# Attention values: six half-width products, three of them on 64 of the 128 rows of TensorE

## The chip, the cores and the metric

The kernel runs on one NeuronCore of a Trainium2 chip. The metric is the device time of one execution in microseconds (us). All data are fp32. The engines have short names in the profile: PE is the matrix engine (TensorE), PEld its weight loads, DVE the VectorE, ACT the ScalarE, POOL the GpSimd engine, and SP the engine whose queue issues the DMAs.

## The reference

The kernel computes one macaron block over 4 sequences of 256 tokens with 512 features: a feed-forward part at half weight, an attention part, and the feed-forward part again. Cut to what matters here:

```python
x = x + 0.5 * ffn(layernorm(x))
# attention, 32 query heads, 8 key/value heads of 128, window of 128 tokens
q, k = rope(x_n @ wq), rope(x_n @ wk);  v = x_n @ wv
allowed = (j <= i) & (j > i - 128)
attn = softmax(where(allowed, q @ k.T * sm_scale, neg))
x = x + (attn @ v) @ wo
x = x + 0.5 * ffn(layernorm(x))
```

The change is in the line `attn @ v`.

## The kernel before, in words

The tokens are worked on in two halves `h` of two sequences `b` each. For every half and every key/value head `g` there is a group of four query heads; each of the 16 groups has two units (b = 0 and b = 1), so there are 32 units. The projections are done in Strassen's manner: seven products of half size and additions on DVE and POOL (`sums_a`, `sums_b`, `queries`, `keys`, `project_values`, `outputs`). The order of PE, DVE, POOL and ACT instructions is written out by hand for most of the kernel: for each unit the main loop runs the steps of the next group's queries (letters in `order`), the scores of the next unit, the output products of the previous unit (`late`), the mask, and `values` at the end. DMAs are issued by SP in an order of the scheduler's.

In a unit, the queries of one sequence (256 tokens) are cut into 8 blocks of 32 tokens. `scores` makes scores, `exponentials` and `normalize` the softmax weights in `probs`; the window is folded, so that a query block of tokens 128 to 255 has only 128 key columns: the column of key `k` holds the weight of key `k` or of key `k + 128`, whichever the window allows. `turn_blocks` transposes 32x32 blocks on DVE and writes them to DRAM (`kept`); `fetch` reads them back into `turned` with four DMAs, so that keys lie on the 128 partitions and (head, query block, query) on the free axis. That leaves, for each key partition, 512 columns for the first 128 query tokens and 512 for the second.

`split` (L804) copies the second 512 columns into `part` with the weights of the first key tile set to zero. It runs on POOL for b = 0 and in the last group (an affine select, L807), otherwise on DVE (a product with the constant mask `new`, L812). `difference` (L817) has replaced the value tile v1 by v1 - v0. `values` (L822) then makes three products of 128 rows and 512 columns each (L829): the first 512 columns with v0 into the bank `oa`, the second 512 with v0 and `part` with v1 - v0 into the bank `ob`. ACT copies each bank to `oT` as soon as it is done (L832); `oT` is read by four additions on POOL (`oTs`, L126) and by the output products `y` on PE (L852), which come in the next unit.

Other names in the prediction: L739 and L753 are the score products `sa` and `sb`, L575 the query products, L742 the masks and maxima of the scores on DVE, L531 the last sum of a rope on POOL, L554 additions of Strassen parts on DVE, L462, L464 and L485 sums of the feed-forward part, `wq`, `wk` and `wv` weight tiles that SP loads.

Of the kernel before, what the change touches and what calls it, by code (L numbers as in the profile page):

```python
# [12 lines left out]
F32 = mybir.dt.float32  # L13
AF = mybir.ActivationFunctionType
ALU = mybir.AluOpType
AX = mybir.AxisListType

P = 128
B, S, D = 4, 256, 512
T = B * S  # L20
NT = T // P
NH, NKV, HD = 32, 8, 128
G = NH // NKV
# [15 lines left out]
def macaron_kernel(  # L39
# [154 lines left out]

    def by_heads(dst, make):
        make(dst, 0)
        other = sb.tile(list(dst.shape), F32, tag="by_heads", bufs=1, name=f"{dst.name}_hi")
        for j in range(1, G):
            make(other, j * BLK)
            nc.gpsimd.tensor_copy(dst[ts(j, BLK), :], other[ts(j, BLK), :])  # L200
# [35 lines left out]
    for c in range(1, NB):  # L236
        nc.gpsimd.memset(turned[ts(c, BLK), :, :c, :], 0.0)


    old = const.tile([P, NB, BLK], F32, name="old")  # L240
    nc.gpsimd.memset(old, 1.0)
    nc.gpsimd.affine_select(
        out=old, in_=old, compare_op=ALU.is_gt,
        fill=0.0, base=0, pattern=[[-BLK, NB], [-1, BLK]], channel_multiplier=1,
    )
    new = const.tile([P, NB, BLK], F32, name="new")
    nc.gpsimd.tensor_scalar(new, old, -1.0, 1.0, ALU.mult, ALU.add)

    rank = const.tile([P, E], F32, name="rank")
    for e in range(E):  # L250
# [103 lines left out]
    def ffn(tiles, tag, then):  # L354
# [22 lines left out]
        def narrow(i):  # L377
            t = tiles[i]
            if i == 0:
                state["hl"] = sb.tile([P, TPH, E * R + E], F32, tag="hl", name=f"hl_{tag}_{t0}")[:, :n, :]  # L380
            pa = score_bank(f"pa_{tag}_{t}")
            for c in range(KC):
                nc.tensor.matmul(  # L383
                    pa[:, : E * R + E], x_of(i, c), ar_sb[:, c, :],
                    start=(c == 0), stop=(c == KC - 1),
                )
            nc.scalar.copy(state["hl"][:, i, :], pa[:, : E * R + E])
# [165 lines left out]
    def add(dst, bank, other):  # L553
        nc.vector.tensor_tensor(dst, bank, other, ALU.add)  # L554
# [111 lines left out]
    def project_values(h, g):  # L666


        x, w = xs[h], weights["vs", h, g]
        dst = sb.tile([P, TPH, 2 * HD], F32, tag="v", name=f"v_{h}_{g}")  # L670
        vS[h, g] = dst
        banks = [mm_bank(f"v{n}_{h}_{g}").rearrange("p (b i f) -> p b i f", b=BPH, i=2) for n in range(2)]
        (c11, c12), (c21, c22) = ((bank[:, 0], bank[:, 1]) for bank in banks)
        (v11, v12), (v21, v22) = (
            (dst[:, :2, cols], dst[:, 2:, cols]) for cols in (slice(0, HD), slice(HD, 2 * HD))
        )
        p1c, u2, v1 = (
            temp(n, f"v_{h}_{g}")[:, :S].rearrange("p (i f) -> p i f", i=2) for n in ("p1c", "u2", "v1")
        )

        def product(n, bank, start=False):
            for i in range(2):
                for c in range(2):
                    nc.tensor.matmul(  # L684
                        bank[:, i, :], x[n - 1][:, c, i, :], w[n - 1][:, c, :],
                        start=(start and i == 0 and c == 0), stop=(c == 1), skip_group_check=True,
                    )

        def first():
            product(1, c11, True)  # L690
            nc.scalar.copy(p1c, c11)
            product(6, c22, True)

        def both():
            add(u2, c22, p1c)

        def second():
            product(5, c12)
            add(v1, c12, u2)
            product(7, c21)  # L700
            add(v22, c21, v1)

        def others():
            product(2, c11)
            product(4, c21)
            add(v21, c21, u2)
            product(3, c12)
            nc.scalar.copy(v11, c11)
            add(v12, c12, u2)
            difference(h, g)  # L710

        return first, both, second, others

# [82 lines left out]
    def fetch(name):  # L796
        heads = kept.pop(name).rearrange("(j k) c x -> k j c x", j=G)
        for c in range(NB):
            nc.sync.dma_start(
                out=turned[ts(c, BLK), :, c:, :].rearrange("p j n q -> p j (n q)"),  # L800
                in_=heads[:, :, c, c * BLK :],
            )

    def split(h, g, b):  # L804
        part = sb.tile([P, G, NB, BLK], F32, tag="part", bufs=1, name=f"part_{h}_{g}_{b}")
        if b == 0 or (h, g) == groups[-1]:
            nc.gpsimd.affine_select(  # L807
                out=part, in_=turned[:, :, NB:, :], compare_op=ALU.is_ge, fill=0.0, base=0,
                pattern=[[0, G], [BLK, NB], [1, BLK]], channel_multiplier=-1,
            )  # L810
        else:
            nc.vector.tensor_tensor(  # L812
                part, turned[:, :, NB:, :], new.unsqueeze(1).to_broadcast([P, G, NB, BLK]), ALU.mult
            )
        return [turned[:, :, :NB, :]], [turned[:, :, NB:, :], part]

    def difference(h, g, tiles=slice(None)):  # L817

        pairs = vS[h, g].rearrange("p (b i) f -> p b i f", i=2)[:, tiles]
        nc.vector.tensor_tensor(pairs[:, :, 1], pairs[:, :, 1], pairs[:, :, 0], ALU.subtract)  # L820

    def values(h, g, b, p0, p1):  # L822
        oT = sb.tile([HD, G, S], F32, tag="oT", bufs=4, name=f"oT_{h}_{g}_{b}")
        v = vS[h, g - g % 2]
        cols = ts(g % 2, HD)
        for i, parts in enumerate((p0, p1)):
            po = (score_bank, mm_bank)[i](f"o{'ab'[i]}_{h}_{g}_{b}")
            for n, part in enumerate(parts):
                nc.tensor.matmul(  # L829
                    po, v[:, 2 * b + n, cols], part, start=(n == 0), stop=(n == len(parts) - 1)  # L830
                )
            nc.scalar.copy(oT[:, :, ts(i, P)], po.rearrange("p (j q) -> p j q", j=G))  # L832
        return oT

    def outputs(h, g, b, oT):
# [162 lines left out]
    def run(queue, n):  # L998
        for _ in range(min(n, len(queue))):
            queue.popleft()()  # L1000
# [24 lines left out]
    for u, (h, g, b) in enumerate(units):  # L1025
# [11 lines left out]
        def turn_half(c):  # L1037
            once(f"t{c}{ahead[-1]}", lambda: turn_blocks(ahead[0], ahead[-1], c))
# [9 lines left out]
        fill(left, 0)  # L1048
        if left == 1:
            nc.scalar.activation(root, eps, AF.Sqrt)  # L1050
        parts = []

        def look_ahead(at=u + 1):
            nonlocal ahead
# [4 lines left out]
            add_sums(h - 1, BPH - 1, nc.gpsimd, slice(-2, None))  # L1059
            sum_weights("v", *groups[n])  # L1060

        def part(at=(h, g, b)):
            parts.extend(split(*at))

        if b == 0 and n < len(groups):

# [4 lines left out]
            steps |= {  # L1071
                "y": lambda: run(late, 1), "r": invert, "n": level, "S": look_ahead,
                "E": lambda: exponentials(*ahead, which=range(NB, 2 * NB)),
                "D": lambda: difference(0, 0, slice(1)),
                "W": lambda: sum_o_weights(h, g, ("t3", "t1")), "X": lambda: sum_o_weights(h, g, ("t2",)),
                "x": between_halves if (h, g) == groups[NKV + 1] else None,
                "V": lambda: sum_o_weights(h, g, ("t4",)), "v": lambda: project_v(0, 0, 2),
                "k": lambda: sum_weights("k", *groups[2]), "a": lambda: fill(left, 1),
                "T": lambda: turn_half(0), "U": turn, "t": part, "c": None, "d": None, "e": None,
            }  # L1080

            if g == NKV - 2 and h + 1 < NHALF:
# [6 lines left out]
        elif b == 1 and n + 1 < len(groups):  # L1089
            both, second, others = begun  # L1090
            both()
            run(late, 1)
            if g == NKV - 2 and h + 1 < NHALF:
                more_tokens[4]()
            level()
            second()
            turn()
            if n == 2:
                for t in behind:
                    measure(t, "a")  # L1100
            if (h, g) == groups[NKV]:
                add_sums(h - 1, b, nc.gpsimd, slice(-2))
            elif n % 2 == 1:
                sum_weights("v", *groups[n + 1])
            others()
            fill(left, 4)
            shifted = [behind.popleft() for _ in range(2 if behind and n in (4, 6) else 0)]
            for t in shifted:
                scale(t, "a")
            if n % 2 == 0 and n + 2 < len(groups):  # L1110
                sum_weights("k", *groups[n + 2])
            if n % 2 == 1 and n + 3 < len(groups):
                load_k(*groups[n + 3])
            elif n % 2 == 0 and n + 2 < len(groups):
                load_v(*groups[n + 2])
            run(late, len(late) - 1)
            for t in shifted:
                norm_attn(t, scaled=True)
        else:
            turn()  # L1120
            run(late, len(late))
            if b == 0:
                sum_o_weights(h, g, ("t3", "t1"))
            fill(left, 1)
# [10 lines left out]
            load_q(*groups[n + 1])  # L1135
        if b == 0 and 1 < n < len(groups):
            load_o(*groups[n])
        if not parts:
            part()
        fill(left, 2)  # L1140
        run(late, len(late) - 1)
        early = ahead[-1] == "{}_{}_{}".format(*units[u + 1]) if left > 1 else False
# [7 lines left out]
        if u == 0:  # L1150
            project_v(0, 0, 3)
            load_v(*groups[2])
        oT = values(h, g, b, *parts)
        if u == 0:
            difference(0, 0, slice(1, 2))
        if b == 0 and n + 1 < len(groups):

# [79 lines left out]
```

## Time and profile before

| | |
|---|---|
| median of 3 runs | 740.98 us (740.31 to 741.28) |
| profiled execution | 740.92 us |
| its span (first to last instruction) | 739.2 us |
| granted TensorE clock in it | 1.000 |
| PE busy | 728.7 us (99%) |
| PEld busy | 603.3 us (82%) |
| DVE busy | 562.5 us (76%) |
| POOL busy | 562.1 us (76%) |
| ACT busy | 195.1 us (26%) |
| copies `oT` L832 on ACT, 64 | 585 ns each |

The profile comes from one execution. The page gives busy time by engine, the chain of work that ended last, and groups of instructions; the timeline gives instructions in order, with start and length in us, engine, line, operation, output and inputs, shape and count, and in brackets the idle time before and what ended it. One product of fp32 data has two weight loads and two records on PE. Their lengths overlap, so the distance between starts, not the length, is what a record costs.

### The profile page before, as it was taken

The numbers are of one execution on the slowest core, as the hardware profiler recorded it, in microseconds if no ns is written. First come the engines' busy times: TensorE is split into PE (matmuls) and PEld (weight loads), VectorE is DVE, ScalarE is ACT, GpSimd is POOL, SyncE is SP. The second block draws the span as 40 slices with busy tenths as digits, with TensorE's granted clock in tenths as the row PEclk, the third lists the DMA queues.
The fourth block names the chain that finished last, engine by engine and source line by source line (L and its number), as shares of the span: only waits on it lengthen the run. The fifth ranks groups of instructions, "written<-read, shape, count | busy, mean of one in ns | idle before, by whom it ended". The sixth has DMA issues, their size and how long they took to land.

```text
span 739.2 us, 11048 instructions
## 1 busy us (share of the span) xinstructions
PE 728.7 (99%) x3606; PEld 603.3 (82%) x3606; DVE 562.5 (76%) x1297; ACT 195.1 (26%) x724; POOL 562.1 (76%) x613
## 2 busy tenths in 40 slices
PE   8999999999999999998999999999999999999998
PEld 6878888888888888886888888888888888888766
DVE  5797895878786878778677867586877867795877
ACT  5520223332222212130222233222123031222331
POOL 6878878777968686859878699868686878976753
PEclk9999999999999999999999999999999999999999
DMA  9301251424245433625142424242332415433201
GB/s 315 141 1 37 89 177 44 155 65 152 92 155 137 149 98 107 186 69 187 53 167 70 137 83 152 81 166 80 118 129 68 150 53 177 116 124 84 71 29 58
DMA packets 78249, 83.58 MB, mean 113 GB/s; under 512 B 21232, under 2 KB 50928, under 8 KB 78192
## 3 DMA queue, kind: packets, MB, share of 16 engines
q1 hardware_dynamic: 78192, 82.87, 35.4%
q8 instruction: 29, 0.48, 0.3%
q14 instruction: 28, 0.23, 0.1%
HBM read 61.88 MB, written 20.97 MB: 112 GB/s over the span
## 4 chain that ended last, share of the span: by engine, by line
PE 84%; POOL 6%; DVE 5%; issue 3%; DMA 1%; SPq 0%; ACT 0%; DVEq 0%; POOLq 0%
PE q L575 24%; PE y L852 22%; PE ob L829 7%; PE v L684 6%; PE k L632 6%; PE sb L753 4%; PE sa L739 3%; PE oa L829 3%; PE p_f L419 3%; PE po_f L419 2%; PE po_f L482 1%; PE y L894 1%; POOL x L393 1%; PE pa_f L383 1%; PE pv L720 1%
## 5 line engine op out<-in xcount | busy, mean ns | idle before, releaser
L531 POOL TENSOR_TENSOR qT<-ra_q,rb_q 128x512 f32<-128x512 f32 x64 | 81.8, 1279 | 74.8 <-DVE rb_q L525 74.8
L525 DVE TENSOR_TENSOR rb_q<-q,sin_sb 64x512 f32<-64x512 f32 x128 | 88.1, 688 | 1.7
L772 ACT ACTIVATE probs<-probs,mx 128x32 f32<-128x32 f32 (+3 forms) x128 | 44.7, 351 | 144.8 <-DVE mx L742 144.8
L779 POOL TENSOR_TENSOR probs<-probs,sm 128x512 f32<-128x512 f32 x64 | 65.7, 1046 | 6.1 <-DVE sm L1031 6.1
L869 DVE TENSOR_TENSOR x<-y,x 128x256 f32<-128x256 f32 (+1 forms) x62 | 34.2, 551 | 41.5 <-PE y L852 41.3
L852 PE MATMUL y<-wot,oT 128*128 128x256 f32 x248 | 63.7, 379 | 0.4 <-DVE rb_q L525 0.4
L852 PE MATMUL y<-wo,oT 128*128 128x256 f32 x248 | 63.7, 379 | 0.0
L832 ACT COPY oT<-oa 128x512 f32<-128x512 f32 x32 | 18.7, 585 | 169.1 <-PE oa L829 169.1
L852 PE MATMUL y<-wo,oTs 128*128 128x256 f32 x244 | 62.6, 379 | 0.0
L575 PE MATMUL q<-xs,wq 128*128 128x256 f32 x256 | 60.6, 379 | 0.2 <-DVE rb_k L525 0.2
L575 PE MATMUL q<-xs,wqs 128*128 128x256 f32 x256 | 60.6, 380 | 0.0
L575 PE MATMUL q<-xa,wq 128*128 128x256 f32 x256 | 60.5, 379 | 0.0
L575 PEld LDWEIGHTS q<-xa,wq 128*128 128x128 f32 x256 | 48.5, 190 | 12.5 <-issue 4.1
L575 PEld LDWEIGHTS q<-xs,wqs 128*128 128x128 f32 x256 | 48.5, 190 | 7.3 <-PE y L852 0.4
L575 PEld LDWEIGHTS q<-xs,wq 128*128 128x128 f32 x256 | 48.5, 190 | 7.0 <-issue 0.5
L791 DVE STREAM_TRANSPOSE probs<-probs 128x512 f32<-128x512 f32 x64 | 43.7, 700 | 10.8 <-POOL probs L779 10.4
L852 PEld LDWEIGHTS y<-wo,oTs 128*128 128x128 f32 x244 | 46.4, 190 | 6.3
L852 PEld LDWEIGHTS y<-wot,oT 128*128 128x128 f32 x248 | 45.8, 190 | 6.5 <-POOL wot L171 0.8
L852 PEld LDWEIGHTS y<-wo,oT 128*128 128x128 f32 x248 | 45.9, 190 | 5.3
L523 DVE TENSOR_TENSOR ra_q<-q,cos_sb 128x512 f32<-128x512 f32 x64 | 43.9, 686 | 6.3 <-PE q L575 2.0
L772 ACT ACTIVATE probs<-sb,mx 128x128 f32<-128x128 f32 x128 | 44.6, 357 | 0.0
L126 POOL TENSOR_TENSOR oTs<-oT 128x256 f32<-128x256 f32 x31 | 22.9, 740 | 23.5 <-ACT oT L832 23.5
(220 smaller groups left out, 1726.7 us busy)
## 6 DMA issues: line engine op xcount, KB each, us to landing
wq<-in_wq_dram SPq DMA_DIRECT2D x16, 1024.0 KB, 5.6
wo<-in_wo_dram SPq DMA_DIRECT2D x16, 1024.0 KB, 5.2
kept<-probs SPq DMA_DIRECT2D x64, 256.0 KB, 2.2
wk<-in_wk_dram SPq DMA_DIRECT2D x8, 512.0 KB, 4.3
wv<-in_wv_dram SPq DMA_DIRECT2D x8, 512.0 KB, 4.1
turned<-kept SPq DMA_DIRECT2D x32, 128.0 KB, 2.6
turned<-kept SPq DMA_DIRECT2D x32, 112.0 KB, 2.9
turned<-kept SPq DMA_DIRECT2D x32, 96.0 KB, 2.6
```

What stands on the lines that cost most here:

```text
L419: nc.tensor.matmul(bank[:, ts(i, D // 2)], lhs[j][m - 1][:, c, :], weights["bs"][m - 1][:, c, :], start=(m in (1, 5, 2, 4) and c == 0), st ...
L523: nc.vector.tensor_tensor(twice(a), twice(src), angle(cos_sb), ALU.mult)
L525: nc.vector.tensor_tensor(twice(b[o : o + half, :]), twice(src[i : i + half, :]), angle(sin_sb[o : o + half, :]), ALU.mult,)
L531: nc.gpsimd.tensor_tensor(dst, view(a), view(b), ALU.add)
L575: nc.tensor.matmul(bank[:, ts(j, S)], w[:, c, ts(j, HD)], x[:, c], start=(new and j == 0 and c == 0), stop=(c == 1), skip_group_check=True,)
L632: nc.tensor.matmul(dst, w[n - 1][:, c, :], x[n - 1][:, c], start=(start and c == 0), stop=(c == 1), skip_group_check=True,)
L684: nc.tensor.matmul(bank[:, i, :], x[n - 1][:, c, i, :], w[n - 1][:, c, :], start=(start and i == 0 and c == 0), stop=(c == 1), skip_group_ ...
L772: nc.scalar.activation(dst, src, AF.Exp, bias=mx[:, n : n + 1], scale=scale, accum_out=sm[:, n : n + 1])
L779: nc.gpsimd.tensor_tensor(w, w, sm.unsqueeze(1).unsqueeze(3).to_broadcast([P, 2, 2 * NB, BLK]), ALU.mult)
L791: nc.vector.transpose(w, w)
L829: nc.tensor.matmul(po, v[:, 2 * b + n, cols], part, start=(n == 0), stop=(n == len(parts) - 1))
L852: nc.tensor.matmul(py[:, ts(i, D // 2)], lhs[n - 1][:, c, :], weights["os", h, g][n - 1][:, c, :], start=(i == 0 and c == 0), stop=(c == 1 ...
```

## The change

The 1024 columns of a unit are cut into four parts of 256 (64 query tokens of four heads each). Call them 1 to 4. Part 1 (tokens 0 to 63) has only keys 0 to 63, so its product takes the low 64 rows alone. Part 2 takes v0 with all 128 rows. Part 3 (tokens 128 to 191) takes v0 with all rows, plus v1 - v0 on the low 64 rows, with the weights of v1 alone. Part 4 (tokens 192 to 255) takes a mixed value tile `vW` (v1 on the low 64 rows, v0 on the high 64) with all rows, plus v1 - v0 on the high 64 rows. So there are six products of 256 columns, three with 128 rows and three with 64. Parts 1 and 3 go to the bank `oa`, 2 and 4 to `ob`.

What else moves with it: `part` is now a constant tile of 256 columns, filled by four further DMAs per unit from `kept` and masked in place, by POOL or DVE as before; `mixture` makes `vW` with two ACT copies of 64 partitions per value tile and stands where `difference` stood; `difference` comes later in DVE's order; both copies to `oT` come after the last product, `oa` first. To make room, some tiles of the start share memory with others.

```diff
+    low, high = slice(0, P // 2), slice(P // 2, P)
...
+    part = const.tile([P, G, NB // 2, BLK], F32, name="part")
...
             add(v12, c12, u2)
-            difference(h, g)
+            mixture(h, g)
...
+        for c in range(NB):
+            n = NB + c - c % 2
+            nc.sync.dma_start(
+                out=part[ts(c, BLK)].rearrange("p j n q -> p j (n q)"),
+                in_=heads[:, :, c, n * BLK : (n + 2) * BLK],
+            )
 
     def split(h, g, b):
-        part = sb.tile([P, G, NB, BLK], F32, tag="part", bufs=1, name=f"part_{h}_{g}_{b}")
-        if b == 0 or (h, g) == groups[-1]:
-            nc.gpsimd.affine_select(
-                out=part, in_=turned[:, :, NB:, :], compare_op=ALU.is_ge, fill=0.0, base=0,
-                pattern=[[0, G], [BLK, NB], [1, BLK]], channel_multiplier=-1,
-            )
-        else:
-            nc.vector.tensor_tensor(
-                part, turned[:, :, NB:, :], new.unsqueeze(1).to_broadcast([P, G, NB, BLK]), ALU.mult
-            )
-        return [turned[:, :, :NB, :]], [turned[:, :, NB:, :], part]
+        engine = nc.gpsimd if b == 0 or (h, g) == groups[-1] else nc.vector
+        engine.tensor_tensor(part, part, new.unsqueeze(1).to_broadcast([P, G, NB // 2, BLK]), ALU.mult)
+
+    vW = {}
+
+    def mixture(h, g, tiles=slice(None)):
+
+        if (h, g) not in vW:
+            vW[h, g] = sb.tile([P, BPH, 2 * HD], F32, tag="vw", name=f"vw_{h}_{g}")
+        pairs = vS[h, g].rearrange("p (b i) f -> p b i f", i=2)[:, tiles]
+        for i, rows in ((1, low), (0, high)):
+            nc.scalar.copy(vW[h, g][rows, tiles], pairs[rows, :, i])
...
-    def values(h, g, b, p0, p1):
+    def values(h, g, b):
         oT = sb.tile([HD, G, S], F32, tag="oT", bufs=4, name=f"oT_{h}_{g}_{b}")
-        v = vS[h, g - g % 2]
-        cols = ts(g % 2, HD)
-        for i, parts in enumerate((p0, p1)):
-            po = (score_bank, mm_bank)[i](f"o{'ab'[i]}_{h}_{g}_{b}")
-            for n, part in enumerate(parts):
-                nc.tensor.matmul(
-                    po, v[:, 2 * b + n, cols], part, start=(n == 0), stop=(n == len(parts) - 1)
-                )
-            nc.scalar.copy(oT[:, :, ts(i, P)], po.rearrange("p (j q) -> p j q", j=G))
+        at, cols = (h, g - g % 2), ts(g % 2, HD)
+        v0, dv = (vS[at][:, 2 * b + i, cols] for i in range(2))
+        w = vW[at][:, b, cols]
+        pa, pb = (make(f"o{c}_{h}_{g}_{b}") for c, make in (("a", score_bank), ("b", mm_bank)))
+        lo, hi = slice(0, S), slice(S, 2 * S)
+
+        def add(dst, v, p, start=False, stop=False):
+            nc.tensor.matmul(dst, v, p, start=start, stop=stop, skip_group_check=True)
+
+        add(pb[:, lo], v0, turned[:, :, 2:4, :], start=True, stop=True)
+        add(pb[:, hi], w, turned[:, :, 6:8, :])
+        add(pa[:, hi], v0, turned[:, :, 4:6, :], start=True)
+        add(pa[:, lo], v0[low], turned[low, :, 0:2, :], stop=True)
+        add(pb[:, hi], dv[high], part[high], stop=True)
+        add(pa[:, hi], dv[low], part[low], stop=True)
+        halves_of = oT.rearrange("p j (i n q) -> p n i j q", i=2, n=2)
+        for n, po in enumerate((pa, pb)):
+            nc.scalar.copy(halves_of[:, n], po.rearrange("p (i j q) -> p i j q", i=2, j=G))
         return oT
...
             run(late, len(late) - 1)
+            if n % 2 == 0:
+                difference(*groups[n])
```

## The prediction

> **What bounds the kernel now.** I read the profile page first: the busy line, the chain that ended last, and PE's own waits.
>
> ```profile
> PE 728.7 (99%) x3606; PEld 603.3 (82%) x3606; DVE 562.5 (76%) x1297; ACT 195.1 (26%) x724; POOL 562.1 (76%) x613
> ...
> PE 84%; POOL 6%; DVE 5%; issue 3%; DMA 1%; SPq 0%; ACT 0%; DVEq 0%; POOLq 0%
> ```
>
> ```profile
> PE ob L829 <- POOL part L807: 1.0, 2, 0.6
> PE k L632 <- DVE v_k L554: 0.8, 1, 0.8
> PE k L632 <- DVE u_k L554: 0.5, 1, 0.5
> ```
>
> The second fence is the list of PE's waits, longest first: total us, times, longest. After the wait for `ident` at the start (1.5 us) these are the longest, all under 1 us, so TensorE hardly ever waits for data. DVE and POOL are busy 76% each and ACT 26%. What PE saves therefore reaches the end until some other engine becomes late.
>
> Next, how PE's time is made up, in the stretch of one unit (b = 1). Columns: start, length, engine, line, tile, count.
>
> ```profile
> 109.98 1.05 PE L739 MATMUL sa<-kT,qT 128*128 128x32 f32 x8
> 110.87 1.25 PE L753 MATMUL sb<-kT,qT 128*128 128x160 f32 x8
> 111.96 1.03 PE L852 MATMUL y<-wot,oT 128*128 128x256 f32 x4
> 112.82 1.03 PE L852 MATMUL y<-wo,oTs 128*128 128x256 f32 x4
> 113.69 1.02 PE L829 MATMUL oa<-turned,v 128*128 128x512 f32 x2
> 114.54 1.02 PE L829 MATMUL ob<-turned,v 128*128 128x512 f32 x2
> 115.40 1.02 PE L829 MATMUL ob<-part,v 128*128 128x512 f32 x2
> 116.26 1.89 PE L575 MATMUL q<-xa,wq 128*128 128x256 f32 x8
> 117.99 0.38 PE L852 MATMUL y<-wot,oT 128*128 128x256 f32 x1
> ```
>
> Each product has two records, so the first starts give the price of one. A record of 512 columns: (116.26 - 113.69) / 6 = 0.428 us. One of 256: (117.99 - 116.26) / 8 = 0.216 us. The `sa` records, of 32 to 128 columns, start (110.87 - 109.98) / 8 = 0.111 us apart whatever their width, so 0.111 us is the floor set by the weight load in front of each record. Above the floor a record costs its columns, and its load is hidden. The values stage takes 6 x 0.428 = 2.57 us per unit, 32 x 2.57 = 82.2 us in all.
>
> **The products.** Before: six records of 512 columns. After: six products of 256 columns, twelve records: three products over 128 keys (6 records, 6 x 0.216 = 1.30 us) and three over 64 (6 records). If 64 rows cost the same as 128 and nothing overlaps, that is another 1.30 us and nothing is gained: columns are what a record costs. The gain can come only from overlap. The three half products use rows low, high, low and banks `oa`, `ob`, `oa`. Within a half the records must follow each other, but the first high record may run beside the second low one, and the second high one beside the third low one: six records in four places, 4 x 0.216 = 0.86 us. The weight loads allow it: 6 x 0.111 = 0.67 us. Saving: 2 x 0.216 = 0.432 us per unit, 32 x 0.432 = 13.8 us. No row of before has a matmul on part of the rows, so the bounds are 0 and 13.8 us. I take 13.8: the halves share neither rows nor bank, and nothing in the rows makes them wait for each other.
>
> **Entering and leaving the halves.** PE changes from whole array to halves and back once per unit: 64 changes. Before shows no such change. Changes of form between `sa`, `sb` and `y` cost 0 to 3 ns in the rows above, the lower bound. The upper bound: PE finishes the record under way (its length 592 ns less the 428 ns to the next start = 164 ns) and only then loads weights (load to product is 0.21 us: the first `sa` load starts at 109.76, its product at 109.98): 164 + 215 = 379 ns. A middle row: after a real stall the second record of a pair comes 533 ns after the first (336.38 us into the span) instead of 428, so a load that is not hidden costs 105 ns. I take 40 ns, nearer to the changes of form in an unbroken stream than to a stall: 64 x 0.040 = +2.6 us, with 0 and 64 x 0.379 = 24 us as ends.
>
> The Trainium skill speaks against this part: "TensorEngine Tiling (Array Packing)", section Tiling Modes, says that changing the tiling mode drains the TensorE. By that rule the change would cost at least the 164 ns tail at each of 64 places, 10.5 us of the 13.8, if the next load stays hidden. No row of before shows it. On the other side, "TensorE: Matmul & The Clock Gate", Part 3, says that products on different row groups run at once, about 4 ns apart; by that the saving is the whole 13.8 us. No row here shows that either.
>
> **The mask on `part`.** The mask works on 256 columns in place of 512. On DVE this was L812, x15, mean 1.03 us; 128x256 additions of the same engine (L554) take 0.42, so some 9 us of DVE leave, off the path. On POOL L807 took 0.73 us and a 128x256 addition (L126) takes 0.73: nothing. These hide under PE.
>
> **Four more DMAs per unit.** They go on SP behind the four of `turned`.
>
> ```profile
> 147.54 1.74 SPq L799 DMA_DIRECT2D turned<-kept  x4
> ...
> turned<-kept SPq DMA_DIRECT2D x32, 80.0 KB, 2.5
> ```
>
> Four take SP 1.74 us and one lands 2.5 us after its issue, so `part` lands some 1.74 us later than `turned` does. In this, one of the tightest b = 1 units (mask done 0.97 us before its product), the last is issued at 147.54 + 7 x 0.435 = 150.6 and lands by 153.1; the mask ends by about 153.9. The first product that reads `part` comes at 153.22 + 7 x 0.216 = 154.7. It holds with 0.8 us. Behind the waiting mask on DVE stand the score masks and maxima (L742), which wait at most 0.1 us longer than now, since L812 ends at 153.97 today. In b = 0 units POOL waits with the mask some 2 us longer; queued behind it is the rope sum L531, which now idles 2.5 to 3 us for DVE, so the wait lies in that idle time, and the mask there is now done some 5 us before PE needs it. If that cover were gone, `qT` and the next scores would be late by the difference. SP's loads behind (`wv`, `wq`) move by 1.74 us in a unit of 20.
>
> Only the last units have no such cover. At 699.35 `turned` is issued and POOL waits 5.84 us for it, masking at 703.37; `part` now lands near 705.2, and behind it on POOL are L462 and L464, whose sums DVE needs (L485) before the last norms. I charge 0.7 us there, between 0 and 2.
>
> **Copies and the mixed tile.** Both `oT` copies (585 ns each) now follow the last product, since `oa` ends last and is copied first: 0.16 + 2 x 0.585 = 1.4 us after the products instead of about 0.8. The first reader on PE is the `y` product behind 1.73 us of other work, so 0.3 us is left; if ACT is late, each 0.1 us is 3 us over 32 units. The next exponentials start 0.6 us later, inside the 5 us. The mixed tile adds two 64-partition copies per `v` tile, about 0.59 us each by the 512-column copy, and `difference` waits for them, but it now stands behind two DVE sums (0.7 us each). ACT idles at 26% busy: nothing.
>
> **The sum.** Profiled execution: 740.9 us, of which 739.2 span, and the median of three runs is 741.0, so no shift. 740.9 - 13.8 + 2.6 + 0.7 = 730.4 us.
>
> **The rivals.** *Dear changes of mode.* The halves overlap, but at each change PE drains and reloads. Place: the first half product and the first product after the stage, both in PE's queue. It decides from 216 ns per change, where 64 x 0.216 takes back the 13.8 us. At 379 ns it is 740.9 - 13.8 + 24.3 + 0.7 = 752.1; a middle of 300 ns gives 747.0, slower than before. For it: a load that is not hidden does cost 105 ns after a stall, and the 164 ns tail is real. Against it: PE goes through all its other changes of form without a gap.
>
> *No overlap.* The halves run one after the other, so the change doesn't do what it says: twelve records of 0.216 us equal the old six of 0.428. 740.9 + 0.7 = 741.6; with 40 ns per change, 744.2. For it: no row of before shows two products at once. Against it: disjoint rows and banks.
>
> **How the numbers follow.** Overlap with cheap changes (0 to 107 ns each): 0.48, 727.8 to 734.6, best guess 730.4. Overlap with dear changes (107 to 379 ns): 0.30, 734.6 to 752; a third of it still faster by over 0.2%. No overlap: 0.22, 741 to over 750, a fifth of it within 0.2%. A difference under 0.2%, 1.5 us, can't be told from none. Faster: 0.48 + 0.10 = 0.58. Same: 0.04 + 0.04 = 0.08. Slower: 0.34. The likeliest case's own range is 727 to 735. The range for 8 in 10 goes from 726.5 (free changes, and the stall for L812 at 631 us gone) to 749, which leaves out the dearest changes (0.06), a drain without overlap (0.09) and little below.
>
> **What would show it.** Right: in PE's timeline the six records on 64 rows span about 0.86 us, their starts in close pairs in the middle, and the stage from its first start to the next product's is 2.2 to 2.4 us instead of 2.57. A record that starts over 0.3 us after its forerunner at the first half product or after the last one shows the dear change; starts 0.216 us apart throughout show no overlap. PE's waits should hold no `part` or `oT` over a few tenths before the last units; DVE's time falls by some 9 us and ACT's rises by some 9. It is wrong altogether if PE waits for `part` in every unit.

## The result and the profile after

| | before | after |
|---|---|---|
| median of the runs beside each other | 741.13 us (740.31 to 741.34, 4 runs) | 744.93 us (744.81 to 745.18, 4 runs) |
| profiled execution | 740.92 us | 744.81 us |
| its span | 739.2 us | 743.0 us |
| granted TensorE clock in it | 1.000 | 1.000 |

The ratio is 1.0054, with a 95% interval of 1.0036 to 1.0071. The change costs 3.8 us where 10.5 us less were forecast. The time lies inside the range of the prediction, on the other side of no change.

The page of the kernel after, the busy line and the chain by engine and by line:

```profile
PE 728.5 (98%) x3798; PEld 621.8 (84%) x3798; DVE 557.3 (75%) x1297; ACT 202.8 (27%) x742; POOL 557.6 (75%) x614
...
PE 82%; POOL 6%; DVE 5%; issue 4%; DMA 1%; SPq 1%; ACT 1%; DVEq 0%; POOLq 0%; ACTq 0%
```

PE was busy 728.7 us before and is busy 728.5 us now: its work hardly became shorter, and its share of the span fell, so there are new holes. The list of PE's waits after (total, times, longest) names them:

```profile
PE ob L842 <- DMA turned<-kept: 2.1, 1, 2.1
PE idle L192 <- POOL ident masks.py:199: 1.5, 1, 1.5
PE k L636 <- DVE rb_q L529: 1.5, 1, 1.5
PE y L914 <- ACT oT L852: 1.2, 1, 1.2
PE p_f L423 <- ACT oT L852: 0.8, 1, 0.8
PE y L872 <- DVE rb_q L529: 0.7, 1, 0.7
```

Each wait happens once. None of them comes back in every unit. The one for `ident` was there before, with 1.5 us, and one for `rb_q` in front of a `y` product with 0.4 us; the others are new. So there are two questions: why the 32 units save nothing, and what the single waits cost.

The first is answered by PE's timeline in the unit that the prediction showed (b = 1 of the first group). Columns as there; `128*128` and `64*128` are the rows and columns of the array that the record uses:

```profile
114.28 0.59 PE L842 MATMUL ob<-turned,v 128*128 128x256 f32 x2
114.71 0.59 PE L842 MATMUL ob<-turned,vw 128*128 128x256 f32 x2
115.14 1.00 PE L842 MATMUL oa<-turned,v 128*128 128x256 f32 x3
115.68 0.48 PE L842 MATMUL ob<-part,v 64*128 64x256 f32 x1
115.99 0.38 PE L842 MATMUL oa<-turned,v 64*128 64x256 f32 x1
116.00 0.38 PE L842 MATMUL ob<-part,v 64*128 64x256 f32 x1
116.20 0.59 PE L842 MATMUL oa<-part,v 64*128 64x256 f32 x2
116.73 0.92 PE L579 MATMUL q<-xa,wq 128*128 128x256 f32 x3
```

A record of a product on 128 rows is called full here, one on 64 rows half, and going from one kind to the other is a change of mode. The third line holds two full records (115.14 and 115.36) and the first half record, at 115.67. So the six half records start at 115.67, 115.68, 115.99, 116.00, 116.20 and 116.42: four places, as forecast. The overlap is real. But after the last full record the first half record comes 0.309 us later instead of 0.216, and the next pair another 0.32 us later. The same happens on the way out: 0.305 us from the last half record (116.42) to the first `q` record (116.73), and 0.32 us to the second. Each change of mode costs some 0.09 us in the first distance (0.093 in, 0.089 out) and 0.104 us in the second, 0.195 us in the mean. The unit pays 0.39 us for a saving of 0.432 us.

Even the rest of 0.04 us is not all gained against the kernel before. Twelve records of 0.2158 us are 2.590 us, while the six old ones, from 113.685 to 116.260, took 2.575 us. What is left is 0.026 us per unit.

The weight loads of the same unit show what PE waited for:

```profile
115.15 0.19 PEld L842 LDWEIGHTS oa<-turned,v 128*128 128x128 f32 x1
115.67 0.18 PEld L842 LDWEIGHTS oa<-turned,v 64*128 64x128 f32 x1 [0.33 <-issue]
...
116.72 0.30 PEld L579 LDWEIGHTS q<-xa,wq 128*128 128x128 f32 x2 [0.33 <-issue]
```

At each change the load unit stands idle for 0.33 us, and the first load of the new mode starts only with its own record (115.67, 116.72) and not under the record before, as everywhere else. The view of line L842 over the whole span (idle time of its engines, times) shows that this one unit stands for all 32:

```profile
  issue: 11.2, 34
```

11.2 us in 34 places is 0.33 us each time, on the way in alone. The starts say the same: there are 33 ways in (the first unit of the last group has two), and in each the first half record starts 0.309 or 0.310 us after the last full one.

The second question is answered by lining up the records of PE that both kernels have, and taking how much later each comes after the change:

```
time before, us    lag of after, us
 99.7              -0.26
101.25             +0.61   first unit: +0.87 at the first y product
165.5              +0.97   falls by 0.025 per unit from here
314.0              +0.77
343.4              +0.78   +1.71 at 338.2 (k products), given back within 5 us
592.9              +0.75
633.0              +0.22   -0.61: the stall of before for L812 is gone
674.6              +0.13   30 of 32 units are behind: level with before
690.0              +0.63   b = 0 of the last group
691.7              +2.31   the feed-forward product p_f
707.5              +3.82   the output projection
```

After 30 units the two kernels are level. The whole loss of 3.7 us lies in the last two units. There PE stands like this after the change:

```profile
688.18 0.67 PE L842 MATMUL ob<-turned,v 128*128 128x256 f32 x2 [2.11 <-DMA turned<-kept]
...
691.24 1.03 PE L423 MATMUL p_f<-wbs_wk,xs_f 128*128 128x256 f32 x4
692.20 0.48 PE L842 MATMUL ob<-part,v 64*128 64x256 f32 x1
...
693.69 1.13 PE L423 MATMUL p_f<-wbs_wk,xs_f 128*128 128x256 f32 x4 [0.79 <-ACT oT L852]
...
710.79 1.12 PE L914 MATMUL y<-wo,oT 128*128 128x512 f32 x2 [1.16 <-ACT oT L852]
```

Before, the two places looked like this:

```profile
686.45 1.10 PE L829 MATMUL oa<-turned,v 128*128 128x512 f32 x2 [0.50 <-issue]
...
706.22 1.02 PE L829 MATMUL ob<-part,v 128*128 128x512 f32 x2
707.08 1.45 PE L894 MATMUL y<-wo,oT 128*128 128x512 f32 x3
```

In the first of the two units PE waits 2.11 us for `turned`, where it waited 0.50 us before. The products on `part` then stand behind eight `p_f` records, so that this unit changes its mode four times instead of twice, and the next `p_f` product waits until ACT has copied `oa` and its bank is free. In the last unit nothing is left to run between the products and the output projection. ACT's copies there, before and after:

```profile
705.56 0.58 ACT L832 COPY oT<-oa 128x512 f32<-128x512 f32 x1 [2.93 <-PE oa L829]
707.28 0.59 ACT L832 COPY oT<-ob 128x512 f32<-128x512 f32 x1 [1.13 <-PE ob L829]
```

```profile
709.67 0.59 ACT L852 COPY oT<-oa 128x512 f32<-128x512 f32 x1 [4.72 <-PE oa L842]
710.15 0.59 ACT L852 COPY oT<-ob 128x512 f32<-128x512 f32 x1
```

Before, `oa` was copied at 705.56 while PE still worked on `ob`, and the projection could start on it at 707.08. After, both copies come behind the last product, and PE waits 1.16 us.

### The profile page after: what moved, and what is told of

The parts are those of the page before. It is cut to its first block, busy times and chain, and to the rows that moved or that the text cites. A ratio compares the mean times of both kernels' runs of the same rounds, so it can differ in the third digit from the quotient of the medians.

```text
span 743.0 us, 11695 instructions
## 1 busy us (share of the span) xinstructions
PE 728.5 (98%) x3798; PEld 621.8 (84%) x3798; DVE 557.3 (75%) x1297; ACT 202.8 (27%) x742; POOL 557.6 (75%) x614
## 4 chain that ended last, share of the span: by engine, by line
PE 82%; POOL 6%; DVE 5%; issue 4%; DMA 1%; SPq 1%; ACT 1%; DVEq 0%; POOLq 0%; ACTq 0%
PE y L872 23%; PE q L579 23%; PE k L636 6%; PE v L688 6%; PE oa L842 5%; PE sb L757 4%; PE ob L842 4%; PE sa L743 3%; PE p_f L423 3%; PE po_f L423 2%; PE po_f L486 1%; DVE rb_q L529 1%; PE y L914 1%; DMA kept<-probs 1%; PE pa_f L387 1%
## 5 line engine op out<-in xcount | busy, mean ns | idle before, releaser
L529 DVE TENSOR_TENSOR rb_q<-q,sin_sb 64x512 f32<-64x512 f32 x128 | 88.1, 688 | 1.7
L579 PE MATMUL q<-xa,wq 128*128 128x256 f32 x256 | 62.1, 386 | 0.0
```

The source lines that it names most:

```text
L529: nc.vector.tensor_tensor(twice(b[o : o + half, :]), twice(src[i : i + half, :]), angle(sin_sb[o : o + half, :]), ALU.mult,)
L579: nc.tensor.matmul(bank[:, ts(j, S)], w[:, c, ts(j, HD)], x[:, c], start=(new and j == 0 and c == 0), stop=(c == 1), skip_group_check=True,)
```

## The experiments

The theory: the overlap is real, and the changes of mode eat it. The rivals: only the overlap is real, or only the gaps are; or the halves hardly overlap and a change of mode costs little. The first three runs tell these apart.

**All six products on 128 rows.**

```diff
-        add(pa[:, lo], v0[low], turned[low, :, 0:2, :], stop=True)
-        add(pb[:, hi], dv[high], part[high], stop=True)
-        add(pa[:, hi], dv[low], part[low], stop=True)
+        add(pa[:, lo], v0, turned[:, :, 0:2, :], stop=True)
+        add(pb[:, hi], dv, part, stop=True)
+        add(pa[:, hi], dv, part, stop=True)
```

> The changed kernel with all six products on 128 rows; the three half products then also take the rows that they should leave out, so the values are not the reference's. No change of mode and no overlap is left. Theory (overlap saves 0.432 us per unit, the two changes of mode cost 0.197 us each, read from the record starts): 32 x 0.038 = 1.2 us longer than the changed kernel, 746.1 us, and the values stage at 12 x 0.216 = 2.59 us. Rival 1 (the gaps around the half products are an artefact of the record, and only the overlap is real): 744.9 + 13.8 = 758.7. Rival 2 (the overlap is an artefact, the gaps are real): 744.9 - 12.6 = 732.3.

Measured: 746.91 us (746.52 to 748.10), ratio to before 1.0078 (1.0061 to 1.0094). That is 2.0 us more than with the halves, and in the trace the lag against the kernel after grows by 0.04 us per unit between 165 and 330 us, which makes 1.3 us over 32. Halves with their changes of mode are worth almost nothing against six plain products. The theory stands, and the two rivals with numbers in the expectation fall. The last rival, no overlap and cheap changes, would have given nearly the time of after, so this run alone doesn't exclude it; the next one does.

**One product alone on 64 rows.** Nothing can overlap, but both changes of mode are there.

```diff
         add(pa[:, lo], v0[low], turned[low, :, 0:2, :], stop=True)
-        add(pb[:, hi], dv[high], part[high], stop=True)
-        add(pa[:, hi], dv[low], part[low], stop=True)
+        add(pb[:, hi], dv, part, stop=True)
+        add(pa[:, hi], dv, part, stop=True)
```

> Only the product of part 1 stays on 64 rows, the other two take 128, so the values are not the reference's. One entry and one exit per unit, and nothing to overlap with. Theory (0.197 us per change of mode): 32 x 0.394 = 12.6 us over the kernel without halves, 758.7 us. Rival (a change of mode costs 0.04 us, as predicted, and the gaps belong to the switching between the two halves): 2.6 us over it, 748.7 us.

Measured: 759.07 us (758.84 to 760.51), ratio 1.0247 (1.0232 to 1.0263). Against the run before this is 759.07 - 746.91 = 12.2 us for 64 changes, 0.19 us each. Timeline of the same unit:

```profile
115.58 1.22 PE L842 MATMUL oa<-turned,v 128*128 128x256 f32 x4
116.73 0.70 PE L842 MATMUL ob<-part,v 128*128 128x256 f32 x2
117.26 0.59 PE L842 MATMUL oa<-part,v 128*128 128x256 f32 x2
117.69 1.67 PE L579 MATMUL q<-xa,wq 128*128 128x256 f32 x7
```

From the first `oa` start to the first `ob` start stand four records, 4 x 0.216 = 0.86 us without changes; it is 116.73 - 115.58 = 1.15 us. The two `ob` records take 117.26 - 116.73 = 0.53 us instead of 0.43. The total is 0.29 + 0.10 = 0.39 us for the two changes, as in the kernel after. This settles the price.

**Order low, low, high.** Both low products come before the high one in the program.

```diff
         add(pa[:, lo], v0[low], turned[low, :, 0:2, :], stop=True)
-        add(pb[:, hi], dv[high], part[high], stop=True)
         add(pa[:, hi], dv[low], part[low], stop=True)
+        add(pb[:, hi], dv[high], part[high], stop=True)
```

> The same six products, but the half ones in the order low, low, high. Theory 1 (each half of the rows takes its own records as soon as it is free, whatever their place in the program, as the first high record starting beside the first low one suggests): still four places, 744.9 us, within 0.5. Theory 2 (products start in program order, and only neighbours overlap): five places, 32 x 0.216 = 6.9 us more, 751.8 us.

Measured: 748.07 us (746.05 to 750.07), ratio 1.0095 (1.0070 to 1.0119); the profiled execution took 746.05 us. The median lies half-way between the two numbers, but the timeline decides against the rival:

```profile
115.86 0.48 PE L842 MATMUL ob<-part,v 64*128 64x256 f32 x1
116.17 0.38 PE L842 MATMUL oa<-turned,v 64*128 64x256 f32 x1
116.18 0.38 PE L842 MATMUL ob<-part,v 64*128 64x256 f32 x1
116.39 0.59 PE L842 MATMUL oa<-part,v 64*128 64x256 f32 x2
116.91 0.70 PE L579 MATMUL q<-xa,wq 128*128 128x256 f32 x2
```

It is the same picture as after: the first high record starts beside the first low one, though four low records precede it in the program, and the six take four places. In the trace the lag against the kernel after stays at +0.03 us from 160 to 638 us and then rises by 1.0 us at a wait for the `xn_f` transfer; at the end it is 1.2 us. One issue of `xn_f`, at 633.48 us, takes 1.66 us where its neighbours take 0.44 to 0.54, beside a 16 KB record of the kind that the run with three old units brings up. Two of the other executions, 749.39 and 750.07 us, had a mean granted clock of 0.995 against 0.999 and 1.000 in the two short ones. 0.5% of 748 us is 3.7 us, about what they took longer; why the clock fell in them isn't known.

**The upper bank copied first.** This undoes the order of the copies, not their place.

```diff
-        for n, po in enumerate((pa, pb)):
+        for n, po in ((1, pb), (0, pa)):
```

> The changed kernel with the two copies to oT swapped: ob first. Theory (with ob copied last its PSUM bank comes free later, so that other tiles get banks that a rope still reads: PE's waits of 0.9 us in the first unit and of 1.7 us at the half boundary): those waits go, some 1 to 1.5 us less, 743.6 us. Rival (the order of the copies does not matter, all of the loss is in the last two units): 744.9 us.

Measured: 743.93 us (743.21 to 749.15, 8 runs), ratio 1.0052 (1.0032 to 1.0071). The medians differ by 1.0 us, which is not to be told from nothing by the spread of all eight. But three of the eight (744.89, 746.75 and 749.15 us) had a mean granted clock of 0.998 to 0.990; the other five, at 0.999 and over, took 743.21 to 744.04 us, all below the shortest execution of after, 744.81 us. The trace is clear as well. First `y` product in the first unit, after and here:

```profile
101.87 1.10 PE L872 MATMUL y<-wot,oT 128*128 128x256 f32 x4 [0.71 <-DVE rb_q L529]
```

```profile
101.10 1.03 PE L872 MATMUL y<-wot,oT 128*128 128x256 f32 x4
```

The reading: PSUM banks are given in the order in which they come free. In the kernel after, `ob` comes free last, and this `y` gets the bank of a `q` product that a rope on DVE (L529) still reads. With `ob` free first it gets that one, as before the change. The views name the rope as what ended the wait, but they don't name banks, so the path by way of the bank is inferred. The wait is gone with 0.88 us; the one of 1.5 us at 338 us stays and is given back, as it was.

The swap does more than that. The kernel after falls behind the one before by 0.40 us between 156 and 166 us and by 0.29 us between 557 and 563 us, in steps of 0.1 us at `q` products. With `ob` first the kernel gains 0.55 and 0.39 us on after in the same two stretches, and the version with two old units gains there too when its copies are turned round. By 638 us the run is 1.7 us ahead of after. So this loss as well comes from the order of the copies; no single wait there is long enough for the list of waits, and which bank it is isn't shown.

**The last two units in the old form.** Three products of 512 columns, the wide mask on POOL, each copy behind its own bank.

```diff
+        if (h, g) == groups[-1]:
+            v = vS[at]
+            for i, parts in enumerate(([turned[:, :, :NB, :]], [turned[:, :, NB:, :], wide[b]])):
...
+                nc.scalar.copy(oT[:, :, ts(i, P)], po.rearrange("p (j q) -> p j q", j=G))
+            return oT
```

> The changed kernel, but the two units of the last group keep the values of before (three products of 512 columns, each bank copied as soon as it is done, no part DMAs; the wide mask tile lies where the query weights were). Theory (30 units level with before, the loss is in the last two, 0.4 + 1.6 + 1.4 us): 744.9 - 3.4 = 741.5 us. Rival (the loss is spread over all units): 744.9 less 2/32 of 3.8, 744.7 us.

Measured: 742.34 us (741.79 to 743.68, 7 runs), ratio 1.0023 (1.0012 to 1.0033). That is 2.6 us under the kernel after. In the trace the steps of 1.6 and 1.4 us at `p_f` and at the output projection are gone. The lag is +0.03 us at 674 and +0.85 us from 690 on, for PE still waits 1.9 us there for `turned`. So the loss of the last group comes from the form of the last two units, all but 0.8 us.

**The last unit alone in the old form.** The same edit under `(h, g, b) == last`.

> Only the very last unit keeps the values of before. Theory (in the last unit both copies to oT come after the products and the output projection waits for the second): 744.9 - 1.4 = 743.5 us. Rival (the projection is late for the extra DMAs of the unit before): 744.9 us.

Measured: 744.21 us (743.27 to 747.03, 5 runs), ratio 1.0053 (1.0037 to 1.0070). It lies between the two expectations and decides nothing by its time. Its trace comes from the longest of its executions, 747.03 us at a mean clock of 0.994, so only the step at the output projection is read from it: 0.35 us instead of 1.40.

**Two old units and the upper bank first.**

> Last group as before, and ob copied first in the other units. Theory (the two gains add: 3.4 for the last two units, 1.5 for the first unit's bank): 744.9 - 4.9 = 740.0 us, which is at or just below the kernel before. Rival (the two losses overlap in the end): 741.5 us.

Measured: 740.94 us (739.71 to 742.62, 11 runs), ratio 1.0004 (0.9995 to 1.0013). Both repairs add up: the kernel is back at the time of before. In the trace it runs 1.0 us ahead of before at 674 us, loses that at 690, where PE still waits 2.1 us for `turned`, and stays level from there on.

**Three old units and the upper bank first.** The same edit, for the unit before the last group as well.

> The last three units (the last group's two and the one before them) take the old form with the wide mask tile, and the upper half's bank is copied first everywhere else. In the version with two old units TensorE still waited 2.1 us for the turned weights in the first unit of the last group, and its records fell from 1.0 us ahead of the kernel before to 0.9 us behind it there. If that wait comes from the later copies of the unit before (theory), it goes to the 1 us or less that the kernel before has, and the time falls by about 0.9 us against the version with two old units: 740.0 us, 0.8 us below the kernel before. If the wait comes from something else, such as the part transfers of the earlier units, the time stays at 740.9 us.

Measured: 740.31 us (739.52 to 742.44, 12 runs), ratio 0.9991 (0.9982 to 1.0000). (The version with two old units was level with before at 690 us, not 0.9 us behind it as the expectation has it.) The time is near the theory's number, but the theory fell: PE's wait for `turned` is 1.9 us, hardly less, so the late copies of the unit before were not its cause. The issues of `turned` on SP show something else. View of the tile `turned` in the last group, after and in the next run but one; the columns are the least, median and greatest length of an issue in ns, and the first and last start in us:

```profile
L803 SPq DMA_DIRECT2D turned<-kept x4: 318/405/1469, 683.3 to 685.6; - x4
```

```profile
L805 SPq DMA_DIRECT2D turned<-kept x4: 303/366/432, 681.7 to 683.2; - x4
```

In the kernel after, one issue of four takes 1.47 us. At 683.58 us, just before it starts, the trace has one of the 31 records of 16 KB of the queue that the page lists as `q8 instruction`. In the kernel before, the nearest ones are at 667.3 and 694.9. All five versions so far in which the last group was changed or the copies were turned round have the long issue too, each with such a record within 0.2 us of its start.

**Other work ahead of the first stage, in the kernel after.** It is meant to move those records and change no stage.

```diff
-    for n in range(20):
+    for n in range(32):
+        nc.tensor.matmul(idle[0:1, 0, 0:1], eps, eps, start=True, stop=True)
+    for n in range(14):
         nc.tensor.transpose(idle[:, n % KC, :], ident, ident)
```

> The changed kernel with other work ahead of the first stage: 32 products of one element on TensorE before the 20 turns of the identity, of which 14 stay; nothing else is changed, and no result uses them. It gives TensorE about 116 instructions more before the stages. In the trace of the changed kernel one of the 16 KB instruction records of queue q8 begins at 683.58 us, 0.07 us before an issue of a turned transfer that takes 1.47 us instead of the 0.40 us of its neighbours, and TensorE waits 2.1 us for turned in that unit; in the kernel before, the nearest such records are at 667.3 and 694.9 us. Theory: these records load TensorE's instructions and come earlier by some 11 us here, to where SyncE issues nothing; the issue takes 0.4 us, the wait for turned falls to about 1.0 us, and the time by about 1.0 us to 743.9 us. Rival: the long issue comes from the queue of transfers itself, it stays, and the time is 744.9 us.

Measured: 744.80 us (744.47 to 745.51, 5 runs), ratio 1.0048 (1.0036 to 1.0061). The nearest such records now stand at 665.8 and 696.2 us, the four issues of `turned` took 1.91 us instead of 2.79, and PE's wait in front of the `ob` products fell from 2.11 to 1.27 us; it is now put down to DVE (`l_f`) and no longer to `turned`. The time did not follow: the first stage ends 0.5 us later, and in the last group a `p_f` product now waits 0.57 us for a DVE maximum (`mx`). A moved record also meets another issue of `turned`, at 506.01 us, which now takes 1.06 us, and PE starts the products of that unit 0.35 us later. The record's part in the long issue is as the theory had it, the time is the rival's.

**The same, with three old units and the upper bank first.**

> The version with the last three units in the old form and the upper half's bank copied first, with the same 32 products of one element ahead of the first stage and 14 turns of the identity instead of 20. That version took 740.3 us, with an issue of turned of 1.69 us at 681.99, beside a q8 record at 682.11. Theory: the record moves, the wait for turned (1.9 us) falls to about 0.8 us, and the time to 739.3 us, 1.8 us below the kernel before. Rival: 740.3 us.

Measured: 739.92 us (739.17 to 741.09, 11 runs), ratio 0.9982 (0.9973 to 0.9991). PE's waits:

```profile
PE k L638 <- DVE rb_q L531: 1.5, 1, 1.5
...
PE oa L852 <- DMA turned<-kept: 0.6, 1, 0.6
```

The wait for `turned` fell from 1.9 to 0.6 us, as expected; of the time 0.4 us came by the medians, and 0.7 us by the ratios. This version beats both kernels, by 1.4 us the one before.

## Why the prediction was wrong

**What held.** A record costs its columns and not its rows: away from the changes, half records of the same rows start 0.216 us apart, as full ones do. The six half records share four places in all units but four (at 336 and 632 us and in the last group, where the products on `part` come late). So the overlap of 0.432 us per unit is right, though the pairs are others than forecast (first low with first high, not second low with first high). The 13.8 us are 0.5 us too many as a saving on the kernel before, for the prediction took twelve short records as equal to six long ones: 32 x 0.0145 = 0.5 us. In the middle units PE waits for `part` once, 0.4 us, and never for `oT`; a `part` transfer lands 2.1 us after its issue (2.5 was taken). The stall of before for L812 is gone, with 0.61 us.

**The step that failed: the changes of mode.** They were put at 40 ns each, "nearer to the changes of form in an unbroken stream than to a stall". They cost 195 ns: 64 x 0.195 = 12.5 us instead of 2.6. With this price alone the prediction's own sum gives 740.9 - 13.8 + 12.5 + 0.7 = 740.3 us, no gain to speak of. The prediction's sign for dear changes, a record over 0.3 us after its forerunner at both ends of the half products, is what the timeline shows. The rows that were taken as nearest (`sa`, `sb`, `y`) change the shape of a product but never the part of the array that it uses, and under them the next load runs ahead. Here it doesn't. The other row in the text, 105 ns for a load that isn't hidden, was the right one for half of the price; the 0.104 us measured is the same thing. The rival "dear changes" named the mechanism and its place, and 195 ns lies in its band of 107 to 379 ns. It is a little less than the 216 ns that take back the whole overlap, which is why the middle of the kernel came out level and not slower.

The Trainium skill, "TensorEngine Tiling (Array Packing)", section Tiling Modes, speaks of a drain when the mode changes. The runs agree that a change costs time, with 0.19 us from two kernels and 0.195 us from the trace. Whether the array empties first they don't show: the first load of the new mode starts 0.307 us after the start of the last full record, whose length the trace gives as 0.379 us. The prediction had weighed that rule and gone by the other rows. "TensorE: Matmul & The Clock Gate", Part 3, has products on different row groups start about 4 ns apart, and the trace shows 7 ns. It also has products start in the order of the program; here a high record starts 0.31 us ahead of a low record that precedes it in `kernel.py`, and the run with the order low, low, high shows it again. In the unit at 336 us, where `part` is late, the same low record starts ahead of the high one, so the order of starts is not that of the instructions in one of the two cases. There the measurement decides.

**The second term that was mis-sized: the last units.** They were put at 0.7 us (0 to 2) for a late `part`. They cost 3.7 us. Late `part` products are one piece of it; the others were not in the sum at all: the copy of `oa` loses its cover in the last unit (1.16 us of PE's wait), the bank of `oa` is held longer in the unit before (0.79 us), that unit has two changes of mode more (0.39 us), and one issue of `turned` is long.

**Not foreseen.** Copying `ob` last costs 0.87 us at the first `y` product and 0.7 us in two stretches of the middle.

Together: 9.9 us for the changes of mode, 3.0 for the last units, 1.6 for the order of the copies, 0.5 for the twelve records in place of six, less 0.6 for the stall. That is 14.4 us, as much as lies between forecast and result (3.9 + 10.5, on the profiled executions); the terms are rounded, and a piece of 0.2 us could hide among them. The terms for copies and mask hid as forecast, though the 128x256 masks on DVE took 753 ns in the mean instead of 420, and DVE fell by 5 us instead of 9; ACT rose by 7.7 us, also off the path.

## What to carry to other kernels

Count the changes between whole-array and part-array products, and set them against the records that the overlap hides: here a change costs about 0.2 us and a hidden record of 256 columns saves 0.216 us, so one hidden record per change gains next to nothing. When a nearest row is chosen for a price, it has to share the property that changes: products of other shapes say nothing of products on other rows. And where a copy loses its cover, look at the first and the last unit by themselves, where the work that hides it elsewhere is missing.

## What the runs showed of the hardware

- The two halves of the rows run out of program order against each other: the first high record starts 7 ns after the first low one and 0.31 us before the second low one. Records of one half keep their order.
- In this stream of products with 256 columns, a change of mode costs PE 93 ns (in) or 89 ns (out) before the next record starts, and then 104 ns of a load that isn't hidden.
- SP's issue of a DMA takes 1.2 to 2.3 us instead of 0.3 to 0.5 where it meets a 16 KB record of the `q8 instruction` queue. In the kernel after, from 100 us on, all ten issues of over 0.9 us start within 0.6 us of such a record. More PE instructions ahead of the first stage moved the records, and the long issue of `turned` was gone in both runs. That the records load PE's instructions fits this but isn't shown. Whether an issue meets one follows from where the records happen to fall, so a difference of 1 us between two versions can be no more than that.
- In one execution (the last unit alone in the old form) the granted clock fell to one half after PE had waited 2.1 us for `turned`. Busy time by window, with the clock in the column before the DMA share:

```profile
688.00:690.00 2.00, 1.79 (x6) 1.07 (x6) 1.93 (x14) 0.00 (x0) 1.21 (x3) 0.82 0.15 33
690.00:696.00 6.00, 6.00 (x15) 3.53 (x14) 3.04 (x10) 0.00 (x0) 2.49 (x2) 0.50 0.00 0
```

  The kernel after waited as long and kept its clock in the profiled execution, so such a wait doesn't lower the clock each time; that it was the cause here is not shown.
